# Load order, temporary tiles and a 36-key half step in a two-layer cross-attention kernel

## The chip, the cores and the metric

The kernel runs on one NeuronCore of a Trainium2 chip. Its time is the device time of one launch in microseconds. Three runs of the kernel before took 598.75, 599.59 and 599.96 us, so its median is 599.59 us.

## The reference

Two cross-attention layers are computed one after the other in float32. There are B = 8 batches, T = 100 queries of width E = 1024, and S = 1444 keys of width L = 512; both layers attend to the same keys.

```python
# layer 0
Q = query @ Wq + bq; K = key @ Wk + bk; V = key @ Wv + bv      # (8,100,1024), (8,1444,1024), (8,1444,1024)
weights = softmax(Q @ K^T / sqrt(1024))
x = query + (weights @ V) @ Wo + bo
# layer 1: on x, with its own weights; softmax over the queries (axis 1), not over the keys
q = x @ Wq + bq; k = ctx @ Wk + bk; v = ctx @ Wv + bv
w = softmax(q @ k^T / sqrt(1024), axis=1)
y = w @ v + x
out = (y - mean(y)) * rsqrt(var(y) + 1e-6) * gamma + beta
```

## The kernel before

The kernel never forms the keys or values of width 1024. It multiplies the weights first (qk is Wq times the transpose of Wk, vo is Wv times Wo), so that the queries are taken into the 512 features of the context and all work per key has width 512. The products of weights use a scheme of sums and fewer multiplications; the TensorE work of all of them is recorded at line 164. Some of these products need sums of scaled rows: `transferred_sum` makes scaled copies on ScalarE into temporary tiles (`scaled_sum`, line 579) and adds them up pairwise with accumulating transfers that GpSimd issues (`transfer_added`, line 574). Among the temporary tiles are the three tiles of the tag "prob", which later hold context features.

Then each layer goes through the batches.

- **Scores.** `scores_by_keys` (matmul at line 934) holds the 1444 keys as 11 blocks of 128 and a last one of 36. For each of the 4 feature chunks (k) and each key block (m) it multiplies the transposed features of the block by the queries. A block of 128 is done as two halves of 64 columns (h), which lie in the two halves of the PE array's columns and write to PSUM partitions 0 to 63 and 64 to 127. The block of 36 has one half only, always h = 0. So a round over the blocks has 23 matmuls, and a batch has 92. Each matmul is two passes in the profile[...].
- **Softmax.** `softmax0` and `softmax1` turn the scores of a batch into weights w, on VectorE (line 97 of the profile is the helper through which all of these go) and ScalarE. They go through the groups of key blocks in ROWS. `softmax0` reduces each group of the PSUM banks to a maximum per query, shifts and exponentiates, and leaves the division for later; `softmax1` scales each group and adds a bias, and normalises every key over the queries, so that its groups are independent of each other.
- **Weighted rows.** `weighted_rows` (A, matmul at line 891) multiplies the weights by the rows of the context, in 48 steps of two column halves.

`alternated(b)` interleaves, step by step, the weighted rows of batch b with the scores of batch b + 2. The scores of batches 0 and 1 are computed first, by `first_scores`. For batch 0 of layer 0 the first round of batch 2's scores goes ahead of the first A step.

The context comes in two forms. `load_features(b)` loads four chunks of transposed features, cT_b_0 to cT_b_3, each in two transfers (line 861). Chunks 0 and 1 take tiles of the tag "unit" (10 buffers), chunks 2 and 3 tiles of "prob" (3 buffers). `load_rows(b)` loads four row tiles c_b_0 to c_b_3 (lines 872, 875, 876), all of "unit". All of these transfers are issued by SyncE, whose queue is served in order: a load that waits for its buffer holds back those behind it.

The order of TensorE's instructions is written out by the program. That of the other engines is chosen by a scheduler, save for instructions under `tc.keep_in_program_order` and those of the Vector helper while its flag `in_order` is set. The loads of the context were under no such order, and in layer 0 the scheduler put batch 1's chunk 2 ahead of its chunks 0 and 1, and its chunk 3 behind the four row tiles of batch 0 and the first two feature chunks of batch 2.

Of the kernel before, what the change touches and what calls it, by code (L numbers as in the profile page):

```python
# [31 lines left out]
P = 128  # L32
# [10 lines left out]
GT = G * T  # L43
SETS = (range(0, 4), range(4, 7), range(7, 8))
LATER = {(1, 5): 4, (1, 7): 4}
ROWS = [range(0, 4), range(4, 8), range(8, 11), range(11, 12)]
LAST = (MC - 1) * P
PAD = S - LAST + QD
SCALE = 1.0 / math.sqrt(E)
# [4 lines left out]
def two_layer_cross_attention(ctx: ExitStack, tc: tile.TileContext, a: dict, out: bass.AP):  # L54
# [11 lines left out]
    def bank(name):  # L66
        return psum.tile([P, 512], F32, tag="ps", name=name)
# [479 lines left out]
    def transferred_sum(name, srcs, of):  # L547

        n = EC if of == "qk1" else EC // 2
        tiles = [row(f"{name}_{n}") for n in range(2)] + [weight_rows(f"{name}_2")[:, :E]]
        tiles += [t[:, :E] for t in prob]
        if of != "qk0":
            tiles += [weight_rows(f"{name}_{n}")[:, :E] for n in range(6, 8)]
        scaled_sum(tiles[:n], srcs[:n])

        def second_half():
            t = tiles[n]  # L560
            if of != "qk0":
# [290 lines left out]
        tc.keep_in_program_order(nc.scalar.activation(xT[:, e, :], xT[:, e, :], AF.Identity, bias=bias))  # L852


    def load_features(b):

        for k in range(LC):
            name = f"cT_{b}_{k}"
            t = feature_block(name) if k >= LC // 2 else unit(name)[:, :S]
            for part in (slice(0, LAST // 2), slice(LAST // 2, S)):  # L860
                nc.sync.dma_start(out=t[:, part], in_=a["ctxT"][b][k * P : (k + 1) * P, part])
            yield t

    def load_rows(b):

        src = a["ctx_512"][b]
        for q in range(NQ):
            t = unit(f"c_{b}_{q}").rearrange("p (c l) -> p c l", c=CQ)
            n = CQ - (q == NQ - 1)
            r0 = q * CQ * P  # L870
            for i in range(n):
                nc.sync.dma_start(out=t[:, i, :], in_=src[r0 + i * P : r0 + (i + 1) * P, :])
            if n < CQ:
                more = PAD - (S - LAST)
                nc.sync.dma_start(out=t[: S - LAST, n, :], in_=src[LAST:S, :])
                nc.sync.dma_start(out=t[S - LAST : PAD, n, :], in_=src[:more, :])
            yield t

    def keys(m):

        return P if m < MC - 1 else S - LAST

    def weighted_rows(s, layer, c, dst):

        b, w = s["b"], s["w"]
        ps = bank2(f"A{layer}_{b}")
        for m in range(MC):
            r = max(keys(m), PAD)
            for k in range(LC):
                for h in range(2):  # L890
                    nc.tensor.matmul(  # L891
                        ps[h * HP : (h + 1) * HP, k * T : (k + 1) * T],
                        c[m // CQ][:r, m % CQ, k * P + h * HP : k * P + (h + 1) * HP],
                        w[:r, m, :],
                        start=(m == 0 and k == 0),
                        stop=(m == MC - 1),
                        skip_group_check=True,
                    )
                if (m, k) == (MC - 1, LC - 1):
                    src = ps[:, :GT].rearrange("p (c t) -> p c t", t=T)  # L900
                    if layer:
                        nc.scalar.copy(dst, src)
                    else:
                        divided(s, ps, dst, src)
                yield

    def divided(s, ps, dst, src):

        for h in range(2):
            nc.tensor.matmul(  # L910
                ps[h * HP : (h + 1) * HP, GT : GT + T],
                ones[:, h * HP : (h + 1) * HP],
                s["wsum"],
                start=False,
                stop=True,
                skip_group_check=True,
            )
        r = work.tile([P, T], F32, tag="rrow", name=f"rrow_{s['b']}", bufs=2)
        nc.vector.reciprocal(r, ps[:, GT : GT + T])
        nc.vector.tensor_tensor(dst, src, r.unsqueeze(1).to_broadcast([P, LC, T]), ALU.mult)  # L920

    def scores_by_keys(s, layer, cT, softmax):

        b = s["b"]
        q = gT[layer][b // G]
        t0 = b % G * T
        banks = [bank(f"s{layer}_{b}_{n}") for n in range(MC // GM)]
        for k in range(LC):
            for m in range(MC):
                for h in range(2):  # L930
                    n = min(HP, keys(m) - h * HP)
                    if n > 0:
                        o = m * P + h * HP
                        nc.tensor.matmul(  # L934
                            banks[m // GM][h * HP : h * HP + n, m % GM * T : (m % GM + 1) * T],
                            cT[k][:, o : o + n],
                            q[:, k, t0 : t0 + T],
                            start=(k == 0 and m % GM == 0),
                            stop=(k == LC - 1),
                            skip_group_check=True,  # L940
                        )
                if (k, m) != (LC - 1, MC - 1):
# [4 lines left out]
        s["softmax"] = softmax(s, [blocks_of(banks, ms) for ms in ROWS])  # L947
        for _ in islice(s["softmax"], LATER.get((layer, b))):
            pass
        yield  # L950
# [7 lines left out]
    def softmax0(s, groups):  # L958

        b, w = s["b"], s["w"]  # L960
        most = work.tile([P, len(groups) - 1, T], F32, tag="most", name=f"most_{b}", bufs=1)
# [12 lines left out]
        spread = turned[:, :, 0, :]  # L974
        vector.tensor_copy(spread, best.unsqueeze(2).to_broadcast([QD, nb, QD]))
        shift = work.tile([P, P], F32, tag="shift", name=f"shift_{b}", bufs=1)
        for q in range(nb):
            vector.transpose(shift[q * QD : (q + 1) * QD, :].rearrange("p (n j) -> p n j", j=QD), spread)
        bias, shift = kb0[:, b * T : (b + 1) * T], shift[:, :T]
        vector.scalar_tensor_tensor(shift, shift, SCALE, bias, ALU.mult, ALU.add)  # L980
        vector.tensor_tensor(shift, bias, shift, ALU.subtract)
        for ms, r, ps in groups:
            n = len(ms)
            rows = w[:r, ms[0] : ms[0] + n, :]
            vector.scalar_tensor_tensor(
                rows, ps, SCALE, shift[:r].unsqueeze(1).to_broadcast([r, n, T]), ALU.mult, ALU.add
            )
            nc.scalar.activation(rows, rows, AF.Exp)  # L988
            yield
        weight_sums(s)  # L990
# [102 lines left out]
        vector.in_order = False  # L1093


    def softmax1(s, scores):

        b, w = s["b"], s["w"]
        groups = []
        for ms, r, ps in scores:  # L1100
            n = len(ms)
            rows = w[:r, ms[0] : ms[0] + n, :]
            bias = kb1[:r, b * T : (b + 1) * T].unsqueeze(1).to_broadcast([r, n, T])
            vector.scalar_tensor_tensor(rows, ps, SCALE, bias, ALU.mult, ALU.add)
            groups.append((ms, r, rows))
            yield
        made = []
# [295 lines left out]
```

## Time and profile before

| what | value |
|---|---|
| median of three runs | 599.59 us |
| the profiled execution, its time | 601.1 us |
| its span, first to last instruction | 599.0 us |
| mean granted clock of TensorE | 0.988 |
| TensorE busy | 580.7 us |
| VectorE busy | 393.5 us |
| ScalarE busy | 133.6 us |
| GpSimd busy | 133.1 us |
| scores of layer 0, busy (line 934) | 116.4 us |
| weighted rows, both layers, busy (line 891) | 232.5 us |
| context rows, issue to landing | 5.5 us (median, 176 transfers of 256 KB) |
| context features, issue to landing | 6.5 and 6.1 us (64 of 370 KB, 64 of 352 KB) |

In the page's second part the span is cut into 40 slices of 14.98 us, so that the fourteenth covers 194.7 to 209.6 us. Digits are tenths of busy time. "SPq" is SyncE's sequencer, "PEld" is TensorE's loading of weights. "idle before <- X" names what ended an idle time. Matmuls overlap, so their mean duration (250 ns) is longer than the distance between them.

### The profile page before, as it was taken

What the parts mean: (1) busy time and instruction counts of PE and PEld (TensorE: products, weight loads), DVE (VectorE), ACT (ScalarE), POOL (GpSimd) and SP (SyncE); (2) the same over time, 40 slices, a digit from 0 to 9 for tenths busy, and PEclk for the clock granted to TensorE, in tenths of its full rate; (3) what the DMA queues carried; (4) which work ended last, traced back from release to release, by engine and by line L of the source; (5) the groups of instructions that cost most, each with busy time, mean ns of one, the idle gap of its engine ahead of it and who ended that gap; (6) DMA issues with size and microseconds to landing.
All of it is one profiled execution on the core that took longest, in us unless ns stands there. A gap on an engine that the chain in (4) does not pass through costs nothing.

```text
span 599.0 us, 17465 instructions
## 1 busy us (share of the span) xinstructions
PE 580.7 (97%) x7470; PEld 503.6 (84%) x7470; DVE 393.5 (66%) x912; ACT 133.6 (22%) x349; POOL 133.1 (22%) x206
## 2 busy tenths in 40 slices
PE   9999999999999499999999999999999999999994
PEld 8887457688899499999997856687999999999992
DVE  1996689888675555774468486885533327663695
ACT  1322320424500102011200000112333303144313
POOL 3110110311210222042223001202931121341052
PEclk9999999999999799999999999999999999999998
DMA  8959999854778999999991004995899992497114
GB/s 275 308 89 349 296 245 310 202 99 97 149 178 263 374 373 370 360 346 358 358 303 54 2 0 143 398 361 188 312 344 361 356 348 94 131 328 258 55 30 82
DMA packets 65096, 142.95 MB, mean 239 GB/s; under 512 B 7548, under 2 KB 12924, under 8 KB 65020
## 3 DMA queue, kind: packets, MB, share of 16 engines
q1 hardware_dynamic: 56574, 117.80, 55.9%
q0 software_dynamic: 8048, 23.57, 18.6%
q8 instruction: 59, 0.97, 0.6%
q10 hardware_dynamic: 398, 0.47, 0.2%
q14 instruction: 17, 0.14, 0.1%
HBM read 121.53 MB, written 6.14 MB: 213 GB/s over the span
## 4 chain that ended last, share of the span: by engine, by line
PE 73%; DMA 9%; issue 4%; POOL 1%; DVE 1%; ACT 1%; SPq 1%; POOLq 0%; DVEq 0%; ACTq 0%
PE A L891 21%; PE s L934 20%; PE o_x L164 5%; PE g_x L164 4%; PE qk_x L164 3%; PE o_y L164 3%; PE g_y L164 3%; DMA g_t<-xT 2%; DMA vo_L_xattn_bv<-vo_L_xattn_bv 2%; DMA cT<-in_ctxT 2%; PE o_w L164 1%; PE o_z L164 1%; PE qk_y L164 1%; PE qk_z L164 1%; DMA c<-in_ctx 1%
## 5 line engine op out<-in xcount | busy, mean ns | idle before, releaser
L891 PE MATMUL A<-w,c 128*64 128x100 f32 (+1 forms) x3072 | 232.5, 250 | 1.3 <-issue 1.3
L891 PEld LDWEIGHTS A<-w,c 128*64 128x64 f32 (+1 forms) x3072 | 205.2, 136 | 3.8 <-issue 3.5
L934 PE MATMUL s<-g0T,cT 128*64 128x100 f32 (+1 forms) x1472 | 116.4, 255 | 8.4 <-DMA cT<-in_ctxT 8.0
L934 PE MATMUL s<-g1T,cT 128*64 128x100 f32 (+1 forms) x1472 | 116.2, 249 | 0.0
L934 PEld LDWEIGHTS s<-g0T,cT 128*64 128x64 f32 (+1 forms) x1472 | 102.2, 139 | 9.3 <-DMA cT<-in_ctxT 8.2
L934 PEld LDWEIGHTS s<-g1T,cT 128*64 128x64 f32 (+1 forms) x1472 | 100.5, 135 | 1.9 <-issue 0.6
L1135 POOL TENSOR_TENSOR part<-w 128x500 f32<-128x500 f32 x16 | 24.5, 1529 | 138.3 <-ACT w L988 64.3
L1115 ACT ACTIVATE w<-w,negmax 128x100 f32<-128x100 f32 x96 | 35.2, 370 | 68.2 <-DVE negmax L97 68.2
L97 DVE TENSOR_REDUCE most<-s 128x100 f32<-128x400 f32 (+1 forms) x24 | 12.5, 525 | 44.7 <-PE s L934 44.5
L988 ACT ACTIVATE w<-w 128x400 f32<-128x400 f32 (+2 forms) x32 | 12.0, 444 | 132.3 <-DVE w L97 115.4
L97 DVE SCALAR_TENSOR_TENSOR w<-s,kb 128x400 f32<-128x400 f32 (+2 forms) x32 | 13.8, 462 | 42.0 <-PE s L934 41.8
L164 PE MATMUL qk_x<-qk 128*128 128x256 f32 x128 | 29.7, 380 | 0.0
L164 PEld LDWEIGHTS qk_x<-qk 128*128 128x128 f32 x128 | 23.3, 190 | 3.0 <-ACT qk L438 0.2
L946 POOL MEMSET w<- 68x100 f32 x16 | 3.8, 238 | 72.9 <-PE A L891 41.5
L1195 DVE SCALAR_TENSOR_TENSOR z<-vectors,r,z 100x512 f32<-100x512 f32 x16 | 11.4, 744 | 12.5 <-PE z L1193 12.4
L97 DVE TENSOR_TENSOR w<-w,rtotal 128x400 f32<-128x400 f32 (+2 forms) x32 | 18.8, 587 | 1.1
L1115 ACT ACTIVATION_READ_ACCUMULATOR w<-w,negmax 128x1 f32 x96 | 18.4, 191 | 0.0
L1208 ACT ACTIVATE z<-z,rstd 100x1024 f32<-100x1024 f32 x7 | 8.1, 1151 | 45.4 <-POOL rstd L1206 45.4
L97 DVE TENSOR_TENSOR xT<-xT,o_x 128x400 f32<-128x400 f32 (+1 forms) x32 | 15.9, 540 | 2.7 <-PE o_x L164 2.4
L669 ACT ACTIVATE g1T<-g_x,k 128x400 f32<-128x400 f32 x4 | 2.4, 596 | 60.2 <-PE g_x L164 60.0
L164 PE MATMUL vo_x<-vo 128*128 128x512 f32 x32 | 15.3, 595 | 0.0
L164 PE MATMUL qk_y<-qk_s 128*128 128x256 f32 x64 | 14.1, 379 | 0.0
(432 smaller groups left out, 1037.9 us busy)
## 6 DMA issues: line engine op xcount, KB each, us to landing
c<-in_ctx SPq DMA_DIRECT2D x176, 256.0 KB, 5.5
cT<-in_ctxT SPq DMA_DIRECT2D x64, 370.0 KB, 6.5
cT<-in_ctxT SPq DMA_DIRECT2D x64, 352.0 KB, 6.1
vo<-in_L_xattn_Wo SPq DMA_DIRECT2D x8, 512.0 KB, 8.7
qk<-in_L_xattn_WqT SPq DMA_DIRECT2D x8, 512.0 KB, 6.2
qk<-in_L_xattn_WqT SPq DMA_DIRECT2D x15, 256.0 KB, 4.9
xT<-in_xT SPq DMA_DIRECT2D x2, 1600.0 KB, 24.3
out<-vectors POOLq DMA_DIRECT2D x7, 400.0 KB, 10.4
```

Of the source, the lines that this page charges most:

```text
L97: ins = getattr(nc.vector, op)(*args, **kw)
L164: nc.tensor.matmul(banks[n // per][:, n % per * width : (n % per + 1) * width], lhs[i][:, n * P : (n + 1) * P], rhs[i], start=(fresh and i ...
L669: nc.scalar.activation(dst[g][:, c, :], banks[j][:, :GT], AF.Identity, bias=u[:, c : c + 1])
L891: nc.tensor.matmul(ps[h * HP : (h + 1) * HP, k * T : (k + 1) * T], c[m // CQ][:r, m % CQ, k * P + h * HP : k * P + (h + 1) * HP], w[:r, m, :],
L934: nc.tensor.matmul(banks[m // GM][h * HP : h * HP + n, m % GM * T : (m % GM + 1) * T], cT[k][:, o : o + n], q[:, k, t0 : t0 + T], start=(k ...
L946: nc.gpsimd.memset(s["w"][:PAD, MC - 1, :], 0.0)
L988: nc.scalar.activation(rows, rows, AF.Exp)
L1115: nc.scalar.activation(rows[:, i, :], rows[:, i, :], AF.Exp, bias=negmax[:, i : i + 1], accum_out=total[:, i : i + 1])
L1135: add(part, w[:, 0:5, :], w[:, 5:10, :], ALU.add)
L1195: nc.vector.scalar_tensor_tensor(z[:, half], bv1[j][:T], s["r"], ps[:T, :], ALU.mult, ALU.add)
L1208: nc.scalar.activation(z, z, AF.Copy, scale=rstd)
```

## The change

The change has three parts.

- **Order of the loads.** All loads of features and rows go through `loaded_in_order`, which keeps them in program order.
- **Temporary tiles of one sum.** For the sum named qk1 the eight temporary tiles are permuted, so that the three tiles of "prob" are only sources of the first round of pairwise additions.
- **The block of 36 keys.** It changes its column half from one occurrence to the next. A variable `side` is flipped after each, and the pairs of full blocks (in the weighted rows and the sum's division too) begin on the other half accordingly. The four chunks of a batch are thereby accumulated in two places in PSUM, partitions 0 to 35 and 64 to 99, and the two partial sums (`rest`) are added on VectorE: in `softmax0` by a copy and an addition for each batch, in `softmax1` by a second `scalar_tensor_tensor`. The key blocks are visited in the order KEYS (8, 11, 9, 10, 0 to 7), the groups of the softmax begin with blocks 8 to 10, and the block of 36 is a group of its own (REST).

```diff
-ROWS = [range(0, 4), range(4, 8), range(8, 11), range(11, 12)]
+ROWS = [range(8, 11), range(0, 4), range(4, 8)]
+REST = range(11, 12)
+KEYS = (8, 11, 9, 10, *range(8))
...
+        if of == "qk1":
+            tiles = [tiles[i] for i in (0, 3, 1, 4, 2, 5, 6, 7)]
         scaled_sum(tiles[:n], srcs[:n])
...
+    def loaded_in_order(to, src):
+        tc.keep_in_program_order(nc.sync.dma_start(out=to, in_=src))
...
-                nc.sync.dma_start(out=t[:, part], in_=a["ctxT"][b][k * P : (k + 1) * P, part])
+                loaded_in_order(t[:, part], a["ctxT"][b][k * P : (k + 1) * P, part])
...
-                nc.sync.dma_start(out=t[:, i, :], in_=src[r0 + i * P : r0 + (i + 1) * P, :])
+                loaded_in_order(t[:, i, :], src[r0 + i * P : r0 + (i + 1) * P, :])
...
+    side = 0
+    def both_sides():
+        return side, 1 - side
+    def one_side():
+        nonlocal side
+        side = 1 - side
+        return (1 - side,)
...
-                for h in range(2):
+                for h in both_sides():
...
         for k in range(LC):
-            for m in range(MC):
-                for h in range(2):
-                    n = min(HP, keys(m) - h * HP)
-                    if n > 0:
-                        o = m * P + h * HP
+            for m in KEYS:
+                whole = keys(m) == P
+                n = HP if whole else keys(m)
+                for h in both_sides() if whole else one_side():
+                    o = m * P + h * HP if whole else m * P
+                    to = banks[m // GM][h * HP : h * HP + n, m % GM * T : (m % GM + 1) * T]
+                    if k >= LC - 2 and not whole:
+                        rest.append(to)
...
-            if r == P:
-                vector.tensor_reduce(most[:, g, :], ps.rearrange("p c t -> p t c"), AX.X, ALU.max)
-            else:
-                vector.tensor_tensor(most[:r, g - 1, :], most[:r, g - 1, :], ps[:, 0, :], ALU.max)
+            vector.tensor_reduce(most[:, g, :], ps.rearrange("p c t -> p t c"), AX.X, ALU.max)
+            if g == 0:
+                vector.tensor_copy(last, rest[0])
+                vector.tensor_tensor(last, rest[1], last, ALU.add)
+                vector.tensor_tensor(most[:n, g, :], most[:n, g, :], last, ALU.max)
+        groups = [*groups, (REST, n, last.unsqueeze(1))]
...
+            if r < P:
+                vector.scalar_tensor_tensor(rows[:, 0, :], rest[1], SCALE, rows[:, 0, :], ALU.mult, ALU.add)
```

More of the change, by code (lines that the diff above doesn't have):

```diff
@@ L871, in load_rows @@
             for i in range(n):
-                nc.sync.dma_start(out=t[:, i, :], in_=src[r0 + i * P : r0 + (i + 1) * P, :])
+                loaded_in_order(t[:, i, :], src[r0 + i * P : r0 + (i + 1) * P, :])
             if n < CQ:
                 more = PAD - (S - LAST)
-                nc.sync.dma_start(out=t[: S - LAST, n, :], in_=src[LAST:S, :])
-                nc.sync.dma_start(out=t[S - LAST : PAD, n, :], in_=src[:more, :])
+                loaded_in_order(t[: S - LAST, n, :], src[LAST:S, :])
+                loaded_in_order(t[S - LAST : PAD, n, :], src[:more, :])
             yield t
@@ L907, in divided @@
     def divided(s, ps, dst, src):
-        for h in range(2):
+        for h in both_sides():
             nc.tensor.matmul(
@@ L927, in scores_by_keys @@
         banks = [bank(f"s{layer}_{b}_{n}") for n in range(MC // GM)]
+        rest = []
         for k in range(LC):
-            for m in range(MC):
-                for h in range(2):
-                    n = min(HP, keys(m) - h * HP)
-                    if n > 0:
-                        o = m * P + h * HP
[L934 to L942, printed above, removed]
+            for m in KEYS:
[6 more added lines that the diff above has]
+                        rest.append(to)
+                    nc.tensor.matmul(
+                        to,
+                        cT[k][:, o : o + n],
+                        q[:, k, t0 : t0 + T],
+                        start=(k == 0 and m % GM == 0),
+                        stop=(k == LC - 1 or (k == LC - 2 and not whole)),
+                        skip_group_check=True,
+                    )
+                if (k, m) != (LC - 1, KEYS[-1]):
                     yield
@@ L946, in scores_by_keys @@
         nc.gpsimd.memset(s["w"][:PAD, MC - 1, :], 0.0)
-        s["softmax"] = softmax(s, [blocks_of(banks, ms) for ms in ROWS])
+        s["softmax"] = softmax(s, [blocks_of(banks, ms) for ms in ROWS], rest)
         for _ in islice(s["softmax"], LATER.get((layer, b))):
@@ L956, in blocks_of, with softmax0 @@
         return ms, r, ps.rearrange("p (c t) -> p c t", t=T)
-    def softmax0(s, groups):
+    def softmax0(s, groups, rest):
         b, w = s["b"], s["w"]
-        most = work.tile([P, len(groups) - 1, T], F32, tag="most", name=f"most_{b}", bufs=1)
+        n = keys(MC - 1)
+        last = w[:n, MC - 1, :]
+        most = work.tile([P, len(groups), T], F32, tag="most", name=f"most_{b}", bufs=1)
         for g, (ms, r, ps) in enumerate(groups):
-            if r == P:
-                vector.tensor_reduce(most[:, g, :], ps.rearrange("p c t -> p t c"), AX.X, ALU.max)
-            else:
-                vector.tensor_tensor(most[:r, g - 1, :], most[:r, g - 1, :], ps[:, 0, :], ALU.max)
+            ordered, vector.in_order = vector.in_order, vector.in_order or g == 0
+            vector.tensor_reduce(most[:, g, :], ps.rearrange("p c t -> p t c"), AX.X, ALU.max)
+            if g == 0:
+                vector.tensor_copy(last, rest[0])
+                vector.in_order = ordered
+                vector.tensor_tensor(last, rest[1], last, ALU.add)
+                vector.tensor_tensor(most[:n, g, :], most[:n, g, :], last, ALU.max)
+        groups = [*groups, (REST, n, last.unsqueeze(1))]
         vector.tensor_reduce(top[:, :T], most.rearrange("p g t -> p t g"), AX.X, ALU.max)
@@ L1093, in project0, with softmax1 @@
         vector.in_order = False
-    def softmax1(s, scores):
+    def softmax1(s, scores, rest):
         b, w = s["b"], s["w"]
         groups = []
-        for ms, r, ps in scores:
+        for ms, r, ps in [scores[0], (REST, keys(MC - 1), rest[0].unsqueeze(1)), *scores[1:]]:
             n = len(ms)
@@ L1103, in softmax1 @@
             bias = kb1[:r, b * T : (b + 1) * T].unsqueeze(1).to_broadcast([r, n, T])
+            ordered, vector.in_order = vector.in_order, vector.in_order or len(groups) < 2
             vector.scalar_tensor_tensor(rows, ps, SCALE, bias, ALU.mult, ALU.add)
+            vector.in_order = ordered
+            if r < P:
+                vector.scalar_tensor_tensor(rows[:, 0, :], rest[1], SCALE, rows[:, 0, :], ALU.mult, ALU.add)
             groups.append((ms, r, rows))
```

## The prediction

> **What bounds the kernel now.** I read the page first, then the waits, then the stretch around the one wait of TensorE that is long.
>
> ```profile
> PE 580.7 (97%) x7470; PEld 503.6 (84%) x7470; DVE 393.5 (66%) x912; ACT 133.6 (22%) x349; POOL 133.1 (22%) x206
> PEclk9999999999999799999999999999999999999998
> DMA  8959999854778999999991004995899992497114
> ```
>
> TensorE is busy for 97% of the span. So time is saved by fewer TensorE slots or by removing its idle time; one slice alone, 194.7 to 209.6 us, has a lower clock (7). The context loads keep the DMA engines full from 185 to 310 us, right beside it. The table of waits, then TensorE's timeline (start, length, instruction, idle time before it), name the idle time:
>
> ```profile
> PE s L934 <- DMA cT<-in_ctxT: 8.0, 1, 8.0
> ...
> 184.06 14.63 PE L934 MATMUL s<-g0T,cT 128*64 128x100 f32 x322
> 206.73 6.92 PE L934 MATMUL s<-g0T,cT 128*64 128x100 f32 x91 [8.03 <-DMA cT<-in_ctxT]
> ```
>
> That is the last of four feature chunks of batch 1: batch 0's scores run from 184.80 to 193.04, batch 1's to 198.69, and chunk 3 is not there. The chain of waits shows why: SyncE issues it at 201.03, after row and feature loads for later steps.
>
> ```profile
> 185.66 0.36 SPq L861
> ...
> 188.11 6.53 DMA c<-in_ctx
> 194.64 0.02 issue
> 194.66 6.32 DMA cT<-in_ctxT
> 200.97 0.02 issue
> ...
> 201.03 5.65 DMA cT<-in_ctxT
> 206.69 0.04 issue
> 206.73 1.43 PE s L934 x13
> ```
>
> The table by stretches (length, TensorE busy, clock, DMA share, GB/s) shows the second cost, a clock of half after the stall:
>
> ```profile
> 193.00:198.00 5.00, 5.00 (x119) 1.00 1.04 402
> 198.00:206.70 8.70, 0.70 (x14) 0.73 1.04 357
> 206.70:212.30 5.60, 5.57 (x67) 0.50 1.04 395
> 212.30:217.00 4.70, 4.70 (x112) 1.00 1.04 393
> ```
>
> **What the Trainium skill says.** "TensorE: Matmul & The Clock Gate", Part 1: after an idle window of about 3.4 us the array runs at half rate. The trace agrees: the clock record falls to 0.5 at 202.0, 3.3 us into the idle time, and stays there for 10.24 us. "TensorEngine Tiling (Array Packing)", Key Properties: different tiles load weights and multiply in parallel. The trace agrees for the two column halves: a pair of halves takes 172 ns, two passes of 86 ns each, both lanes at once. "DMA: Bandwidth & Descriptors", Specifications: about 358 GB/s of HBM per core; the stretches between 215 and 300 us average 359. "VectorE: DVE Perf Modes", Why PSUM operands drop a tier: fp32 operands in PSUM get no fast mode; the 36x100 operations at 0.24 to 0.25 us agree with there being nothing to gain by their form.
>
> **Part 1, the order of the loads.** SyncE's stream now has all four chunks of batch 0, then of batch 1, then rows and features in turn. What goes is the 8.03 us stall and the half clock behind it: 5.6 us at 0.5 is 2.8 us of lost work. Together 10.8 us.
>
> What comes instead? Before, SyncE sat from 164 to 183.8 with batch 1's chunk 2 at its head, waiting for a prob buffer. The second part (the reordered temporary tiles of the qk1 sum) frees these buffers with the first additions, around 160 to 164.5 by my reading of the POOL transfers from 154 on. So chunks 0 to 2 of batch 1 (2.2 MB, 6.1 us at 360 GB/s) load before 184, where the page has 149 to 263 GB/s in use. Its price is on ScalarE: the second scaled copy waits for a transfer that lands near 154.3, then seven at 1.04 us end near 161.7, at most 1.5 us later than before; TensorE is on earlier qk products then, so I cost it at nothing. Uncovered it would be those 1.5 us.
>
> Chunk 3 of batch 1 takes the buffer of batch 0's chunk 2, which TensorE frees after three rounds: 184.80 + 3 x 1.975 = 190.7 (round length below). Everything later queues behind it on SyncE: c_0_0, cT_2_0, c_0_1 and so on. The first byte takes 2.66 us, as in the burst at 183.79, then 360 GB/s: chunk 3 (0.74 MB) lands near 195.5 and is needed at 184.80 + 7 x 1.975 = 198.6. Then each row tile (0.79 MB, 2.2 us) and feature chunk (2.05 us): c_0_0 197.6 (needed 202.6), cT_2_0 199.7 (needed 200.6), cT_2_1 203.9 (needed 202.6, when batch 2's first round is done). So a wait of about 1.3 us at cT_2_1, 0.2 at cT_2_2, too short for the clock.
>
> Afterwards one batch is 5.98 MB, 16.6 us at 360 GB/s. TensorE took 16.8 us per alternated batch before (213.4 to 314.3, six of them) and takes 16.5 with part 3. These are equal within my error, so the lead of the loads stays near zero: stepping through the six batches gives 0 us of waits at 363 GB/s, 1.1 at 358, 2.8 at 352, 4.8 at 345, much of it the same wait as the 1.5 above. I take 1.5 us in all, with 0 and 4.8 as ends. In layer 1 the first rows landed at 403 for a need at 424, and even queued behind chunk 3 (free near 406) they land by 415: nothing.
>
> **Part 3, the 36-key half step.** The lone half now alternates between the column lanes, and every pair begins on the lane that is free. The rounds before show what a lone half costs:
>
> ```profile
> L934 PE MATMUL s<-g0T,cT 128*64 128x100 f32 x184 | 8.7, 250 | 0.0
> L934 PE MATMUL s<-g0T,cT 128*36 128x100 f32 x8 | 1.3, 249 | 0.0
> ```
>
> These are batch 0's scores, by shape: 92 matmuls of two passes, four of them lone. The lone steps start 2.060 us apart in the trace (186.004, 188.064), 12 slots of 172 ns: the lone one pays a whole slot. With both lanes always fed it pays its 86 ns. 16 calls x 4 = 64 lone halves x 86 ns = 5.5 us, 2.75 in each layer; a round becomes 11.5 x 172 = 1.975 us. All TensorE instructions stay. The bounds are 0 (lanes do not overlap across the change of side) and 5.5.
>
> The halves must be added on VectorE: 16 operations in layer 0 (a copy at 0.22, an addition at 0.25 for each batch) and 8 in layer 1 at 0.24, 5.7 us of 205 us that VectorE idles. In layer 0 b0's softmax is the tight place: its last multiplication ended at 199.65 and its exponentials at 200.20. It now starts its last reduction 0.35 us earlier, but that is a 0.57 us reduction where there was a 0.25 us step: ready near 200.3. The first A step follows 12 score steps of batch 2, at 202.6. Cover 2.3 us; without it each us late is a us. The buffers of batch 0's scores are read by 199.6, needed from 200.6.
>
> **Sum.** 8.0 + 2.8 + 5.5 - 1.5 = 14.8 us. The profiled execution had a span of 599.0 and a time of 601.1; the median of the runs is 599.59. 599.0 - 14.8 = 584.2 of span; taken off the median, 584.8. I say 585.
>
> **Rivals.** *The lanes do not overlap*, so part 3 gains nothing: 599.6 - 9.3 = 590. Against it: the pairs overlap now. For it: no run shows a pair that begins on lane 1. Partial gains lie between. *The loads become the bound of layer 0*: at 345 GB/s 3.3 us more waits, 588; for it speaks the DMA row of nines, against it the ample lead in the middle of the stretch of before. *The stall only moves*: chunk 3, or cT_2_1 behind it, is late by over 3.3 us, and the half clock returns (up to 10.24 us at half, 5.1 lost): 8.4 to 12 of the gain go, 593 to 597. The estimated spare time of chunk 3, 3.1 us, speaks against it. *The order does not do what it says*, because the prob tiles come free no earlier: then batch 1's chunks start at 184 in order and all four land by about 195, so most of part 1 is still won, about 587. *Slower*: the strict queue drains in every alternated batch of layer 0, since each cT chunk 3 waits for its buffer with all rows behind it. About 5.7 us of transfers are out ahead, so a block shorter than roughly 3 us is free, and past it each costs its excess plus nothing else; 16.3 us over six batches means 2.7 us each, a block of 5.7 us. I count 8.7 us of margin the other way (the buffer is free at three quarters of the batch before, the issue comes a quarter into the next), so the buffer must be 14 us later than I think. The same loss follows from a stream at 311 GB/s, which no full stretch shows (341 to 369). Result about 601 to 603.
>
> **How the numbers follow.** Chances: the forecast with its small waits 0.58 (582 to 588), lanes without gain 0.10 (588 to 591), loads as the bound 0.13 (587 to 591), stall moved 0.08 (592 to 597), prob tiles no earlier 0.04 (586 to 590), slower 0.07. Within 0.2% of before (598.4 to 600.8) only pieces of the last two meet: 0.02. A gain above 16.3 has no source, bar chance in the run, so the low end is 582; the high end of 591 leaves out the moved stall and the slower case.
>
> **What would show it.** Right: no stall of TensorE above 2 us near 199 to 206, clock 1.0 there, SyncE's batch 1 chunks issued near 166 to 171 and its chunk 3 near 190.7; lone halves 1.975 us apart; TensorE at 97% or more. Wrong: several waits of scores on cT between 215 and 315, a slice of PEclk below 9, batch-1 chunks still issued at 184, rounds still of 2.06 us, or waits of A on w.

## The result and the profile after

The changed kernel takes 597.44 us (median of 7 runs, 596.58 to 600.11) where the kernel before takes 599.62 (7 runs). The ratio is 0.9956, with a 95% interval of 0.9935 to 0.9976: 2.6 us faster, where 14.8 were forecast. Measured again with 20 runs the ratio was 0.9957 [0.9937, 0.9977]. The profiled execution took 597.27 us, with a span of 595.5.

The page of the kernel after, the rows that answer to those shown of before:

```profile
PE 576.7 (97%) x7470; PEld 498.1 (84%) x7470; DVE 397.5 (67%) x936; ACT 134.8 (23%) x349; POOL 133.8 (22%) x206
PEclk9999999999999999999999999999999999999999
DMA  8959989943696999999981707709999990699114
```

The slice of clock 7 is gone, and with it the long stall. The table of waits, for TensorE alone, shows what stands in its place:

```profile
PE s L957 <- issue: 3.0, 6, 0.8
PE A L910 <- issue: 2.4, 4, 0.7
PE o_z_x L166 <- DVE xT L99: 1.9, 1, 1.9
PE A L910 <- DVE rtotal L99: 1.5, 1, 1.5
PE s L957 <- DMA cT<-in_ctxT: 1.4, 1, 1.4
```

The wait for cT is 1.4 us, as forecast. Two waits for VectorE are new (xT, rtotal), and "issue", idle time that no semaphore explains, is 5.4 us. Before, it was 1.6:

```profile
PE A L891 <- issue: 1.3, 3, 0.5
PE s L934 <- issue: 0.3, 1, 0.3
```

The stretches around the old stall (length, TensorE busy, TensorE weight loads, VectorE, ScalarE, GpSimd, clock, DMA share, GB/s):

```profile
193.00:198.00 5.00, 5.00 (x122) 5.00 (x120) 4.73 (x14) 0.00 (x0) 0.00 (x0) 1.00 0.98 354
198.00:203.70 5.70, 5.67 (x132) 5.51 (x128) 5.55 (x13) 1.63 (x4) 1.41 (x2) 1.00 1.04 392
203.70:205.30 1.60, 0.25 (x7) 0.06 (x3) 1.60 (x4) 0.00 (x0) 1.36 (x4) 1.00 1.09 410
205.30:212.00 6.70, 6.70 (x150) 6.57 (x152) 6.28 (x19) 0.30 (x1) 0.95 (x3) 1.00 1.03 350
```

One short gap, and the clock stays at 1.00. Batch 1's chunk 3 was issued at 191.7 and landed at 195.9.

To see where the gain went I compared the starts of TensorE's stages in the two traces. The last column shares out the forecast: the stall, the clock and the wait of 1.5 us stand in the second row, the half steps, at 86 ns each, where they are done.

| stage of TensorE | before, us | after, us | difference | forecast |
|---|---|---|---|---|
| start to first scores | 184.06 | 185.48 | +1.42 | 0 |
| first scores to the product of totals k1, two alternated batches later | 60.87 | 50.68 | -10.19 | -10.6 |
| from there to layer 0's first product o_x | 77.64 | 77.80 | +0.16 | -1.5 |
| to the first scores of layer 1 | 77.59 | 79.57 | +1.98 | 0 |
| to the end of the first four alternated batches | 90.70 | 91.91 | +1.21 | -2.0 |
| to the end of the next three | 65.71 | 66.30 | +0.59 | -0.7 |
| to the end | 42.43 | 43.76 | +1.33 | 0 |
| span | 599.0 | 595.5 | -3.5 | -14.8 |

The first row is within the scatter of one kernel: the kernel before, profiled a second time, reached its first scores at 185.69. The second row came out as forecast. From there on the change loses 5.3 us where 4.2 were to be won.

The half step does what it should. In the scores of a batch that run without another batch's weighted rows between them, lone half steps stood 2.06 us apart before; after they stand 1.89 and 2.05 apart in turn, mean 1.975, as worked out. In the alternated batches an undisturbed pair of rounds takes 3.95 + 4.11 us where it took 4.12 + 4.12.

### The profile page after: what moved, and what is told of

Same layout as the page of the kernel before. It is cut to its first block, busy times and chain, and to the rows that moved or that the text cites. A ratio compares the mean times of both kernels' runs of the same rounds, so it can differ in the third digit from the quotient of the medians.

```text
span 595.5 us, 17451 instructions
## 1 busy us (share of the span) xinstructions
PE 576.7 (97%) x7470; PEld 498.1 (84%) x7470; DVE 397.5 (67%) x936; ACT 134.8 (23%) x349; POOL 133.8 (22%) x206
## 4 chain that ended last, share of the span: by engine, by line
PE 92%; issue 3%; DMA 2%; POOL 2%; DVE 1%; ACT 1%; DVEq 0%; POOLq 0%; SPq 0%
PE A L910 21%; PE s L957 20%; PE qk_x L166 7%; PE g_x L166 5%; PE o_x L166 5%; PE vo_x L166 3%; PE o_y L166 3%; PE g_y L166 3%; PE qk_z L166 2%; PE qk_y L166 2%; DMA cT<-in_ctxT 1%; PE o_w L166 1%; PE o_z L166 1%; PE qk_w L166 1%; PE vo_y L166 1%
## 5 line engine op out<-in xcount | busy, mean ns | idle before, releaser
L910 PE MATMUL A<-w,c 128*64 128x100 f32 (+1 forms) x3072 | 229.2, 249 | 3.9 <-issue 2.4
L910 PEld LDWEIGHTS A<-w,c 128*64 128x64 f32 (+1 forms) x3072 | 200.5, 137 | 6.7 <-issue 6.5
L957 PE MATMUL s<-g1T,cT 128*64 128x100 f32 (+1 forms) x1472 | 114.7, 249 | 1.4 <-issue 1.4
L957 PE MATMUL s<-g0T,cT 128*64 128x100 f32 (+1 forms) x1472 | 112.6, 249 | 3.0 <-issue 1.6
L957 PEld LDWEIGHTS s<-g1T,cT 128*64 128x64 f32 (+1 forms) x1472 | 99.0, 136 | 3.5 <-issue 2.8
L957 PEld LDWEIGHTS s<-g0T,cT 128*64 128x64 f32 (+1 forms) x1472 | 97.5, 136 | 4.9 <-issue 2.6
L166 PE MATMUL qk_x<-qk 128*128 128x256 f32 x128 | 31.1, 393 | 0.0
L1228 DVE SCALAR_TENSOR_TENSOR z<-vectors,r,z 100x512 f32<-100x512 f32 x16 | 11.3, 743 | 13.9 <-PE z L1226 13.9
L673 ACT ACTIVATE g1T<-g_x,k 128x400 f32<-128x400 f32 x4 | 2.4, 594 | 61.2 <-PE g_x L166 61.1
L578 POOL DMA_DIRECT2D qk_L_xattn_bk<-qk_L_xattn_bk x6 | 5.2, 922 | 45.4 <-ACT qk_L_xattn_bk L583 18.0
```

The source lines that it names most:

```text
L166: nc.tensor.matmul(banks[n // per][:, n % per * width : (n % per + 1) * width], lhs[i][:, n * P : (n + 1) * P], rhs[i], start=(fresh and i ...
L578: nc.gpsimd.dma_start(out=to, in_=t, accum_op=ALU.add)
L673: nc.scalar.activation(dst[g][:, c, :], banks[j][:, :GT], AF.Identity, bias=u[:, c : c + 1])
L910: nc.tensor.matmul(ps[h * HP : (h + 1) * HP, k * T : (k + 1) * T], c[m // CQ][:r, m % CQ, k * P + h * HP : k * P + (h + 1) * HP], w[:r, m, :],
L957: nc.tensor.matmul(to, cT[k][:, o : o + n], q[:, k, t0 : t0 + T], start=(k == 0 and m % GM == 0), stop=(k == LC - 1 or (k == LC - 2 and no ...
L1228: nc.vector.scalar_tensor_tensor(z[:, half], bv1[j][:T], s["r"], ps[:T, :], ALU.mult, ALU.add)
```

## Experiments

My theory after the comparison: each part works, and the gain is lost in three new waits of TensorE, each with its own cause: xT (the new order of VectorE's work), rtotal (the new order of the softmax groups) and issue (instruction fetches that come late because the loads fill the DMA engines). The rivals: part 3 gains nothing across a batch; VectorE is merely late for its added operations; issue waits are TensorE's own; what is taken from one wait returns in another.

**Each part alone.** The half step alone:

```diff
-        if of == "qk1":
-            tiles = [tiles[i] for i in (0, 3, 1, 4, 2, 5, 6, 7)]
...
     def loaded_in_order(to, src):
-        tc.keep_in_program_order(nc.sync.dma_start(out=to, in_=src))
+        nc.sync.dma_start(out=to, in_=src)
```

> Part 3 alone on the kernel before: no load is ordered, no temporary tile permuted. Theory (each part works as worked out, and the gain is lost in new waits): a round of scores takes 1.975 us, so 5.5 us less TensorE work; the last softmax of layer 1 divides blocks 0 to 3 third, so TensorE waits 1.5 us for rtotal near 568; the stall on cT stays at 8 us or more with its half clock. Sum 599.6 - 5.5 + 1.5 = 595.6, few waits of kind issue. Rival (alternating sides saves nothing across a whole batch): 600 to 601.

It took 600.66 us, ratio 1.0015 [0.9997, 1.0034]: no gain at all. Its TensorE waits:

```profile
PE s L955 <- DMA cT<-in_ctxT: 9.3, 1, 9.3
PE s L955 <- issue: 2.8, 4, 1.0
PE A L908 <- DVE rtotal L99: 1.5, 1, 1.5
...
PE A L908 <- issue: 1.0, 2, 0.5
```

Against the 5.5 us stand 1.3 us more of stall, 1.5 of rtotal and 2.2 more of issue. The stall is the instructive one: chunk 3 comes when its transfer comes, so faster rounds ahead of it only lengthen the wait. The remaining 2 us or so of the difference in span I could not assign to a wait of the profile. My expectation of 595.6 missed, although the reasons named in it are there. (Part 3 also sets `in_order` around VectorE's first operations of each softmax, lines that the diff of the change above does not show; they were not tried apart.)

The loads alone (the kernel before with parts 1 and 2):

```diff
+        if of == "qk1":
+            tiles = [tiles[i] for i in (0, 3, 1, 4, 2, 5, 6, 7)]
         scaled_sum(tiles[:n], srcs[:n])
...
+    def loaded_in_order(to, src):
+        tc.keep_in_program_order(nc.sync.dma_start(out=to, in_=src))
...
-                nc.sync.dma_start(out=t[:, part], in_=...)
+                loaded_in_order(t[:, part], ...)     # the rows likewise
```

> Parts 1 and 2 alone: program order of the loads and the permuted tiles, the half step as before. Theory: stall of 8 us and half clock gone, about 1.5 us of stall at cT_2_1 instead, so 599.6 - 9.3 = 590.3, less what the new order costs elsewhere: VectorE's g_s sums now stand just ahead of the sums into xT and TensorE waits about 2 us for xT near 322, and TensorE waits on instruction issue while the loads fill the DMA engines, 2 to 4 us. Sum 594 to 596, no wait for rtotal. Rival (the issue waits and the late xT come from part 3): 590 to 591.

597.73 us, ratio 0.9965 [0.9944, 0.9987]; 1.7 us above the upper end that I expected. The waits for xT and of kind issue are where I put them:

```profile
PE o_z_x L164 <- DVE xT L97: 2.1, 1, 2.1
PE s L939 <- issue: 1.7, 3, 0.6
PE A L896 <- issue: 1.6, 3, 0.8
```

The wait for xT has a second cost that I had not priced. TensorE's timeline at its end, and the stretch behind it (length, TensorE busy, clock, DMA share, GB/s):

```profile
322.92 0.60 PE L164 MATMUL o_z_x<-o_t,o_t 128*128 128x200 f32 x2 [2.07 <-DVE xT L97]
324.20:327.60 3.40, 3.40 (x36) 0.50 0.02 5
```

The clock fell to half for 3.41 us behind it, which is 1.7 us of work. Of the five profiles with a wait of 1.9 us or more for xT, two have this half clock (this run and the one without the permutation, below); the changed kernel's two have not. So an execution pays 1.9 us or some 3.6 us for the wait.

So the wait for xT belongs to the order of the loads (without the permutation it is there too, 1.9 us), that for rtotal to the half step, and issue waits rise with either. The loads alone are as fast as the whole change, within the intervals: whatever part 3 saves, the full kernel does not show it.

**Without the permutation of the temporary tiles.**

```diff
-        if of == "qk1":
-            tiles = [tiles[i] for i in (0, 3, 1, 4, 2, 5, 6, 7)]
```

> The changed kernel without the permutation of the temporary tiles (part 2 undone); all else as changed. Theory: the prob tiles come free only with the last additions near 184, so batch 1's chunk 2 waits there as before and its chunk 3 and everything behind it are about 6 us of transfers later: chunk 2 lands near 190 and is needed near 196.6, chunk 3 lands near 196 to 197, the first rows and chunks of batch 2 about 1 us later than now, so 0 to 3 us slower than the changed kernel, 597 to 600. Rival (the permutation does nothing for the loads): no difference, and chunk 2 of batch 1 issued before 175.

596.02 us (8 runs), ratio 0.993 [0.9896, 0.9965]: not slower. Chunk 2 of batch 1 did wait for its buffer, issued at 187.7 and landed at 191.7 (with the permutation 173.8 and 183.0), but it was needed only near 197, and chunk 3, which waits for batch 0's scores either way, landed at 195.6 (195.9 with). The permutation frees early a buffer that nothing needs early.

**The wait for xT.** VectorE's timeline of the kernel after (start, length, instruction) shows two additions of the queries' g_s among the sums that o_z_x waits for:

```profile
317.11 1.57 DVE L99 TENSOR_TENSOR g_s<-qk 128x1024 f32<-128x1024 f32 x1
318.60 0.56 DVE L939 TENSOR_TENSOR A0T<-A,rrow 128x400 f32<-128x400 f32 x1
319.08 1.03 DVE L99 TENSOR_TENSOR xT<-xT,o_x 128x400 f32<-128x400 f32 x2
320.04 1.21 DVE L99 TENSOR_TENSOR g_s<-g_s,qk 128x1024 f32<-128x1024 f32 x1
321.18 1.04 DVE L99 TENSOR_TENSOR xT<-xT,o_z 128x400 f32<-128x400 f32 x2
```

Before, these two ran near 309 and 313, well ahead of those sums (o_x starts at 322.57 there):

```profile
308.93 1.43 DVE L97 TENSOR_TENSOR g_s<-qk 128x1024 f32<-128x1024 f32 x1 [4.28 <-PE A L891]
313.06 1.23 DVE L97 TENSOR_TENSOR g_s<-g_s,qk 128x1024 f32<-128x1024 f32 x1 [0.48 <-DMA cT<-in_ctxT]
```

No line of the diff touches them; the scheduler moved them when the loads were ordered. The experiment keeps them behind:

```diff
         if b == B - 2:
+            vector.in_order = True
             for part in parts:
                 run(part)
+            vector.in_order = False
...
+            vector.in_order = bool(layer)      # around each of the three sums S1, S2, S3
             if layer:
                 combine(S1, A21, A22, ALU.add)
```

> The changed kernel, but VectorE keeps the sums into xT ahead of the two g_s sums of layer 1's queries. Theory: the 1.9 us that TensorE waits for xT before o_z_x near 322 are these two operations (1.57 and 1.21 us) in its way; they go, 597.4 - 1.9 = 595.5. Rival (xT is late because batch 7's softmax is late): the wait stays at 1 us or more.

593.97 us (4 runs), ratio 0.9893 [0.985, 0.9937]. The wait is gone from the profile, here in the kernel after and then in this run:

```profile
322.54 0.60 PE L166 MATMUL o_z_x<-o_t,o_t 128*128 128x200 f32 x2 [1.93 <-DVE xT L99]
320.46 0.61 PE L166 MATMUL o_z_x<-o_t,o_t 128*128 128x200 f32 x2
```

Theory held; the median fell by some 3 us, more than the wait. The clock may be the rest: the mean clock of these four executions was 0.997 to 0.998, while over 20 of the changed kernel it lay between 0.993 and 0.998, and 3.41 us at half are 0.003 of the span.

**The wait for rtotal.** In the last batch of layer 1 the weighted rows begin with key block 0. Before, blocks 0 to 3 were the first group to be normalised; after, they are the third, so TensorE waits for VectorE's division. VectorE's timeline of the kernel after, end of the chain (first and third group):

```profile
562.80 0.17 DVE L99 RECIPROCAL rtotal<-total 128x3 f32<-128x3 f32 x1
563.00 0.47 DVE L99 TENSOR_TENSOR w<-w,rtotal 128x300 f32<-128x300 f32 x1
...
566.88 0.17 DVE L99 RECIPROCAL rtotal<-total 128x4 f32<-128x4 f32 x1
567.09 0.57 DVE L99 TENSOR_TENSOR w<-w,rtotal 128x400 f32<-128x400 f32 x1
```

```diff
         made = []
+        groups.sort(key=lambda group: group[0][0])
         for g, (ms, r, rows) in enumerate(groups):
```

> The changed kernel, but softmax1 normalises and divides its groups in the order of their blocks (0 to 3 first) once all are scaled. Theory: the 1.5 us that TensorE waits for rtotal near 568 are due to the order of the groups; they go, 597.4 - 1.5 = 595.9. Rival (VectorE is simply late there because of the added operations): the wait stays at 1 us or more.

The wait is gone, so its cause is the order of the groups and not the number of operations. But the time was 597.53 us, ratio 0.9959 [0.9939, 0.9979]: no gain. The profiled execution (599.36 us) had more issue waits than that of the changed kernel:

```profile
PE s L957 <- issue: 4.7, 10, 0.7
PE A L910 <- issue: 2.7, 5, 1.1
```

Both edits together:

> The changed kernel with both edits: VectorE sums into xT ahead of g_s, and softmax1's groups normalised in the order of blocks. Theory: neither wait of TensorE (1.9 us for xT, 1.5 us for rtotal) is left; 597.4 - 3.4 = 594.0, and what is missing against the forecast of 585 is the waits of kind issue (4 to 7 us in the profile) and 1.5 us of cT. Rival (time saved on one wait comes back as another, as the groups alone showed no gain in the median): 596 to 597 with more issue waits than 5 us.

594.93 us (6 runs), ratio 0.9905 [0.9872, 0.9938]. Neither wait is left, but the edit of the groups adds nothing that the medians show (593.97 with the xT edit alone; the intervals overlap). Issue waits are 5.9 us. The rival, that what is won there returns as issue waits, cannot be excluded for these 1.5 us.

**The issue waits.** One of them at close range, in the kernel after: the DMA queues from 281.0 to 282.4 us, and TensorE's timeline (idle time before the instruction in brackets):

```profile
q1 hardware_dynamic: 277, 0.53, 100.1%
q8 instruction: 1, 0.02, 5.0%
```

```profile
271.46 0.30 PE L957 MATMUL s<-g0T,cT 128*64 128x100 f32 x2 [0.24 <-issue]
277.44 0.30 PE L957 MATMUL s<-g0T,cT 128*64 128x100 f32 x2 [0.35 <-issue]
283.63 0.25 PE L957 MATMUL s<-g0T,cT 128*64 128x100 f32 x1 [0.48 <-issue]
```

The queue q8, named instruction, moves 59 packets of 16 KB in the execution, which is 65 bytes for each of TensorE's 14,940 recorded instructions; I read it as the fetch of TensorE's program, a block of about 256 instructions at a time, 5.5 us of alternated work. In the trace's records such packets start at 268.96, 274.79 and 281.13, and TensorE resumes 2.5 to 2.65 us after each. This is no accident of one place: of the 128 issue waits of TensorE in all 17 traces, 126 end 2.2 to 2.9 us after the start of such a packet. By chance about one in eight would, since a packet comes every 5.7 us or so in the alternated batches.

If I place every packet on TensorE's program (the lone half steps, whose place in the program is known, serve as marks), the packet starts some time after TensorE has entered a new block, and idle times stand behind those that start about 2 us or more after. This lateness, at 21.5 ns an instruction (86 ns for the four of a half step), can be averaged over the alternated batches. It is a reconstruction: a plain count of the recorded instructions gives values up to 0.3 us apart from these, in the same order.

| kernel | mean lateness, layer 0 and 1, us | issue waits, us | SyncE waits on TensorE, layer 0 and 1, us |
|---|---|---|---|
| before | 0.82, 0.72 | 1.6 | 18.4, 59.0 |
| before again | 1.00, 0.84 | 1.1 | 13.5, 61.1 |
| half step alone | 1.17, 1.32 | 3.8 | 18.4, 52.5 |
| after | 1.49, 1.69 | 5.4 | 0.9, 37.4 |
| after again | 1.57, 1.92 | 4.0 | 0.9, 37.4 |
| both edits | 1.57, 1.69 | 5.9 | 0.6, 39.3 |
| both edits, a quarter of the bytes gone | 0.60, 0.65 | 0.5 | 27.1, 59.3 |

The last column, SyncE's waits for TensorE, is what the order of the loads changed. In the alternated part of layer 0, first before, then after:

```profile
SPq L872 <- PE s L934: 11.5, 9, 2.8
SPq L861 <- PE s L934: 6.6, 6, 2.6
```

```profile
SPq L860 <- DMA c<-in_ctx: 22.9, 61, 1.2
SPq L860 <- DMA cT<-in_ctxT: 20.7, 37, 1.0
SPq L860 <- PE s L957: 0.6, 1, 0.6
```

Before, the 8 us stall of TensorE let the loads run ahead, until they had to wait for buffers. After, SyncE hardly waits for a buffer in layer 0, and the loads run at 366 GB/s over these 101 us where it was 352 (362 and 356 in the second profiles of the two kernels). My reading is that the fetch comes late because the loads leave it no pause. The table does not settle that: with the half step alone SyncE waits as long as before and the loads run at 342 GB/s, and yet it has 3.8 us of issue waits; and in layer 1 the changed kernel's fetches are as late although SyncE waits 37 us there. The test takes bytes away from the kernel with both edits. The second part of each feature chunk is not loaded, and key blocks 5 to 11 use the features of blocks 0 to 4:

```diff
-            for part in (slice(0, LAST // 2), slice(LAST // 2, S)):
+            for part in (slice(0, LAST // 2),):
...
-                    o = m * P + h * HP if whole else m * P
+                    o = m % 5 * P + h * HP if whole else 0
```

> As the kernel with both edits, but the second part of every feature chunk is not loaded, and the scores of key blocks 5 to 11 read the features of blocks 0 to 4 in its place, so that the loads are 4.46 in place of 5.98 MB per batch and the output is not the reference's; TensorE has the same instructions. Theory: the issue waits are fetches of TensorE's instructions that come late because the loads fill the DMA engines; with a quarter of the bytes gone they fall below 1.5 us and the wait for cT goes: 594 - 4 - 1.5 = 588 to 589. Rival (issue waits are TensorE's own, whatever the loads do): 592 to 593, issue waits of 4 us or more.

583.78 us, 11.1 less than with all the bytes and below the 588 to 589 that I expected. TensorE's table of waits in full:

```profile
PE warm L111 <- DVE ones L108: 1.1, 1, 1.1
PE A L916 <- issue: 0.5, 1, 0.5
```

So the issue waits do hang on the loads, and are not TensorE's own. (The test takes packets away together with bytes, so it can't tell which of the two counts.) Of the difference in span, 592.5 to 581.8 us, the two tables of waits name 7.4 us: 5.4 of issue, 1.3 of cT, 0.7 of g_t. The other 3.3 us are in no table: rounds that show no wait are slower too (in layer 0 for instance 4.27, 4.24 and 4.16 us where the light kernel takes 4.11, 3.96 and 3.96). Why, these runs do not show.

The same reduction on the kernel before:

> The kernel before with the same part of the loads left out (output not the reference's). Its issue waits were 1.6 us in the one profile; theory: they fall to about 0, and from the first scores of layer 1 on, where there is no stall, this kernel loses to the one with both edits 2.75 us, the 32 half steps of that layer. The stall on batch 1's chunk 3 stays, some 3 to 5 us in place of 8. Time 593 to 597. Rival (the half step is worth less than its 86 ns): the two are less than 1.5 us apart over layer 1.

590.47 us, below the 593 to 597 expected; issue waits 0.4 us. The stall, of which I expected 3 to 5 us to stay, is nearly gone (0.8 us of cT waits): with shorter transfers ahead of it, chunk 3 comes earlier than I reckoned. Per alternated batch of layer 0 the two light kernels differ by 0.34 us (16.67 against 16.33), four half steps. From the first scores of layer 1 on they differ by 1.28 us only, which by my own criterion speaks for the rival. The stages place it: up to the end of the first four alternated batches 1.99 us of the 2.06 worked out if the one issue gap of the faster kernel (about 0.7 us) is set aside, and nothing in the next three batches. There whole-width products (z) stand between the rounds, and a round with one takes 5.27 us in both. Three rounds without one do save 0.33 us together (4.13 + 4.12 + 4.12 in the light kernel before, 3.97 + 4.11 + 3.96 in the other), but the round behind them, with z in it, gives that back (5.28 and 5.63). In sum the forecast's 86 ns for each of the last eight half steps was not there.

A smaller dose, the second part of chunk 1 alone:

```diff
-            for part in (slice(0, LAST // 2), slice(LAST // 2, S)):
+            for part in (slice(0, LAST // 2), slice(LAST // 2, S))[: 1 if k == 1 else 2]:
```

> The kernel with both edits, but the second part of feature chunk 1 alone is not loaded and its scores of key blocks 5 to 11 read the features of blocks 0 to 4 (output not the reference's): 5.60 in place of 5.98 MB per batch, 6% less. Theory (the instruction fetches suffer from the last few per cent of DMA load, since TensorE's 16.4 us per batch need 365 GB/s of some 360): the issue waits fall below 3 us and the time by 4 to 7 us, 588 to 591, more than half of what a quarter of the bytes gave. Rival (in proportion to the bytes): 11.1 x 6/25 = 2.7 us, 592.

591.67 us, 3.3 less for 6% of the bytes, issue waits still 3.9 us. A quarter gave 11.1, so the gain goes about in proportion to the bytes (2.7 expected by that rival). That most of it lies in the last few per cent is not borne out; with 4 runs against 6, and medians of different groups of runs, it is not ruled out either.

The repeats:

> The changed kernel again, unchanged, to have its median and its issue waits a second time beside these. Theory: 597.4 with 4 to 7 us of issue waits; SyncE waits on TensorE for less than 1.5 us of the 101 us of alternated batches in layer 0. Rival (the first profile's 5.4 us were chance): issue waits of 2 us or less, as in the kernel before.

596.81 us (20 runs, 594.26 to 602.1), issue waits 4.0.

> The kernel before, unchanged. Theory: 599.7, its instruction fetches start on average 0.7 to 1.1 us after TensorE has entered a block, issue waits 1 to 2.5 us, SyncE waits on TensorE 18 us in layer 0's alternated part. Rival (the first profile was lucky): lateness of 1.4 us or more and issue waits of 4 us or more, as in the changed kernel.

600.80 us (20 runs), ratio to the other runs of the same kernel 1.0021 [1.0008, 1.0033], which is how far two labels of one kernel can lie apart here; the gain of the change is about twice that. Issue waits 1.1 us, lateness 1.00 and 0.84: with two profiles of each kernel, the difference between them was no accident of one profile.

**Can the order be kept without the loss?** First, layer 1's loads freed of the order, on top of both edits:

```diff
+    loads_ordered = True
+
     def loaded_in_order(to, src):
-        tc.keep_in_program_order(nc.sync.dma_start(out=to, in_=src))
+        load = nc.sync.dma_start(out=to, in_=src)
+        if loads_ordered:
+            tc.keep_in_program_order(load)
...
+    loads_ordered = False
     scores1 = first_scores(0, 1, softmax1)
```

> The kernel with both edits, but in layer 1 the loads are free of program order again, so that rows and features of later steps pass batch 1's chunk 3 there, as in the kernel before. Theory (instruction fetches come late while the load queue is never empty; in layer 1 the strict order lost 5 to 7 us of lead, so SyncE waits less for buffers and the queue stays full): SyncE's waits on TensorE in the alternated part of layer 1 go from 39 us back to 50 or more, TensorE's issue waits there from about 4 us to 1 or less, time 594.9 - 2.5 = 592 to 593. Rival (issue waits there have nothing to do with the order): 594 to 596 and issue waits of 3 us or more in layer 1.

590.07 us (6 runs), ratio 0.9809 [0.9781, 0.9838]. SyncE's waits on TensorE in layer 1 rose from 39.3 to 53.8 us. The profiled execution was its slowest (594.39) and had 3.8 us of issue waits in layer 1, no fewer. The same kernel again, for a more usual execution:

> The kernel with both edits and layer 1's loads free, unchanged, for a profile of a more usual execution. Theory: median 590 to 591.5; issue waits of layer 1 at 1.5 us or less where the profiled execution is near the median. Rival (the gain of the median was chance): median 593 to 595 and issue waits of 3 us or more in layer 1.

590.51 us, and in an execution of 589.99:

```profile
PE A L920 <- issue: 1.7, 4, 1.0
PE s L967 <- DMA cT<-in_ctxT: 1.7, 2, 1.4
...
PE s L967 <- issue: 0.7, 2, 0.5
```

2.4 us of issue waits, 1.7 of them in layer 1; lateness 1.16 and 1.06. The strict order in layer 1 cost 4.5 us of the median. The gain is clear of the intervals in both measurements; that it comes by way of the fetches is supported by this profile and not by the other.

Second, in layer 0 three loads ahead of batch 1's chunk 3:

```diff
-    run(first_scores(1, 0, softmax0))
+    features, rows, later = load_features(1), load_rows(0), load_features(2)
+    f1 = [next(features) for _ in range(3)]
+    c0, f2 = [next(rows)], [next(later)]
+    c0.append(next(rows))
+    f1.append(next(features))
+    started = (chain(c0, rows), chain(f2, later))     # handed to the first alternated()
+    run(scores_by_keys(batches[1], 0, f1, softmax0))
```

> The kernel with both edits, but in layer 0 SyncE issues c_0_0, cT_2_0 and c_0_1 ahead of batch 1's chunk 3, which waits until about 191 for its buffer. Theory: 2.3 MB more are loaded before 191, so the lead of the loads in layer 0 grows by about 6 us; the 1.3 us of cT waits go, SyncE waits on TensorE for some us in place of less than 1, and TensorE's issue waits in layer 0 (2 to 2.5 us, and as much again in slow rounds) fall by half: 594.9 - 1.4 - 1.5 = 592. Rival (the rate of the loads, not their lead, decides): only the cT wait goes, 593.5.

594.86 us: no gain over 594.93. The cT wait is gone as expected, and the loads land some 6 us earlier (c_1_0 at 209.1, not 215.2), but SyncE still waits on TensorE for 3.4 us only, and issue waits are 5.8. By its lead, layer 0 is not cured.

All four edits:

> All four edits together: sums into xT first, groups by block, loads of layer 1 free, chunk 3 behind three loads in layer 0. Theory: the gains add up, 594.9 - 2.5 - 2.9 = 589.5. Rival (what is won from one wait returns as another): 592 or more.

588.90 us (4 runs, 587.38 to 590.8), ratio 0.9797 [0.9765, 0.9829], near the 589.5 expected: the fastest full kernel here, 11 us below the kernel before at its side, 8 below the changed one.

## Why the prediction was wrong

It said 585 with a range of 582 to 591; 597.4 came out. Nearly every sign that it listed for being right was there: no stall above 2 us, clock 1.0 near 199 to 206, batch 1's chunk 3 issued at 191.7, lone halves 1.975 us apart, TensorE at 97%. They were signs that the parts work, and none looked at what the parts would cost elsewhere. By its steps:

- **The stall and the half clock: right.** Forecast 8.0 + 2.8 us gained and 1.5 lost again; the stage came out at -10.19 us against -10.6 with the half steps in it. Chunk 3 was estimated at 195.5 and landed at 195.9; that is close by luck in part. It was issued 1.0 us later than worked out and took 4.2 us, not 4.7: the first packets of the burst at 183.79 start at 184.73 in the trace, 0.94 us after it and not 2.66.
- **The permutation (part 2): right in its mechanism, of no use.** The prediction gave it about 2 us (587 if the buffers came free no earlier). They came free early, but nothing needed them early, and without it the kernel was not slower.
- **The half step: right in size where nothing interrupts** (1.975 us a round; 0.34 us a batch between the light kernels), 0 in sum over the last eight half steps of layer 1, among whole-width products, where 0.7 us had been forecast.
- **The term of 1.5 us for the loads ("I take 1.5 us in all, with 0 and 4.8 as ends"): wrong.** This is the step that failed most. I priced the full DMA engines as waits for cT alone, and as such the term was right: 1.4 us. What I put at nothing without a reason was everything else that the loads can hold up. The price came as issue waits, which I read as late instruction fetches, of 5.4 and 4.0 us in two profiles where it had been 1.6 and 1.1, and as slower rounds beside them; a quarter of the bytes taken away gave 11.1 us, and of these only 1.3 had been waits for cT. My rival "the loads become the bound of layer 0" had the right place, but the wrong form (waits for cT, 4.8 us with the 1.5), and named layer 0 alone. The row "A <- issue 1.3" of the kernel before was on its page, and I passed over it.
- **VectorE's work at no cost ("5.7 us of 205 us that VectorE idles"): wrong twice.** I followed the added operations into layer 0's first softmax and looked no further. In layer 1's last batch the new order of the groups costs 1.5 us of waiting for rtotal. And existing instructions moved: the g_s sums, 1.9 us on xT, with half a clock behind it in two of five profiles. This is also where the prediction's clock was too simple: it called short waits "too short for the clock" and took 3.3 us of idle time for the threshold that the stall showed, but 2 us were enough twice.
- **The rivals.** The queue that drains in each batch of layer 0 did not come about: the opposite did, SyncE hardly had to wait for a buffer (0.6 us).

In the two profiled spans 11.3 us are missing (3.5 gained where 14.8 were forecast). The waits above name 1.9 (xT), 1.5 (rtotal) and 3.8 (issue); the later start of the scores, within the scatter of one kernel, is 1.4, and the half steps among whole-width products 0.7. That leaves some 2 us in slower rounds.

What stays open: why the saving of 1.5 us on rtotal does not show in the medians, why rounds without a wait are slower, why the half step alone already raises the issue waits, and by what rule the fetch loses against the loads.

## What to carry to other kernels

When an engine at 97% is freed of a stall, ask what the stall was giving to others: here it gave the loads a lead, so that they paused for buffers. That those pauses let the instruction fetches through is likely from these runs, but not shown. A change of order must be priced on every engine's queue, the instructions that the diff does not name included; compare the orders before and after line by line around each step that TensorE waits for. Full DMA engines should be priced at more than the visible waits for data; taking some of the bytes away in an experiment tells how much hangs on them.

## What the runs showed of the hardware

The profile's instruction queue moves packets of 16 KB, 65 bytes for each recorded TensorE instruction, and in layer 0's alternated batches of the changed kernel they start 4.4 to 6.3 us apart, 5.7 in the mean. They share the DMA engines with the loads. Nearly all idle time of TensorE that no semaphore explains (126 of 128 waits in 17 traces) ends 2.2 to 2.9 us after the start of such a packet. By the reconstruction above, a packet that starts about 2 us or more after TensorE has entered a block leaves it idle.

How late the packets come does not follow from the mean rate of the loads alone. In layer 0, 366 GB/s went with 1.5 us of lateness and 298 GB/s, with a quarter of the bytes gone, with 0.6. But the half step alone had 1.2 us at 342 GB/s where the kernel before had 0.8 at 352, and in layer 1 295 GB/s went with 1.7 us, over a stretch that holds one pause of the loads of 22 us.

The half clock behind an idle time lasted 3.41, 6.83 or 10.24 us in these traces. It came after the 8 us stall each time, and after a wait of 1.9 to 2.1 us in two profiles of five. The changed kernel's time ranged from 594.26 to 602.1 us over 20 executions. How much of that is fetches and how much is clock is not shown: its two profiles, 597.27 and 597.43 us, had 5.4 and 4.0 us of issue waits and no half clock before the end.
